# A macaron block on one core: the order of side work in the fourth sums stage, and where its last tiles run

## The chip, the cores and the metric

The kernel runs on one core of one Trainium2 chip. The metric is the device time of one execution in microseconds (us); lower is better. Several executions are timed, and their median counts. One more execution is recorded by the hardware profiler, and the tables and timelines below come from that one.

The engines that matter here are TensorE (matmuls and transposes, PE in the profile), ScalarE (activations and copies, ACT), VectorE (reductions and elementwise work, DVE), GpSimd (indirect DMAs, POOL) and SyncE (which issues most DMAs, SP). Each executes its own instructions in order, and they wait for each other by semaphores.

## The reference, cut to what matters

All is float32. There are four sequences of 512 tokens with 512 channels. A mixture-of-experts layer is applied at half weight, then attention, then the same mixture-of-experts layer again.

```python
def block(x):                                    # x: (4, 512, 512)
    x = x + 0.5 * ffn(layernorm(x))
    x = x + attn(layernorm(x))                   # attn returns out + its input
    return x + 0.5 * ffn(layernorm(x))

def attn(X):                                     # 16 heads of 32 channels
    Xn = layernorm(X) * ln_w + ln_b
    Q, K, V = split(Xn @ W_in, 3)                # rotary embedding on the first 16 channels of Q, K
    probs = softmax(Q @ K.T / sqrt(32))
    return (probs @ V) @ W_out + X

def ffn(x):                                      # x flattened to tokens
    scores = sigmoid(x @ gate_w)                 # 64 experts, 6 chosen by group-limited top-k
    topk_w, topk_ids = grouped_topk(scores + bias)
    y = routed(x, topk_w, topk_ids, w_gate, w_up, w_down)
    shared = (silu(x @ ws_gate) * (x @ ws_up)) @ ws_down
    return y + shared
```

The kernel sends the first expert layer, the attention and the second expert layer through the core one after the other. The change lies in the attention part.

## The kernel before, in words

A tile is 128 tokens, so a sequence has four tiles (`TPB` is 4). The attention of sequence `b` has two stages. The sums stage (`sums`) runs over 4 head groups `c` and 4 query tiles `q`, 16 passes. In each, TensorE computes the scores of four heads into two score buffers (L965), VectorE takes the negated row maximum (`nmq`, L968), and ScalarE takes exponentials whose row sums are accumulated (L973). The results of the exponentials are not kept; only maxima and sums are. `logs` turns the sums into logarithms on VectorE and ScalarE (L944 to L953), and `rows_of_sums` transposes them (`ps_m`, `nmT`). The context stage (`context`) runs over 4 head groups and 4 key tiles `kt`, again 16 passes. TensorE computes transposed scores (L995) and adds the stored rows by a second matmul (L999), ScalarE takes exponentials into `pT` (L1006), and one pass later TensorE multiplies by the values into `cx` (L1018). Score buffers come from `psS`, which has three of two banks each. A sums or a context pass uses two of them.

Beside these passes runs side work. It lies in one queue, `work`, an instance of `Pieces`. A piece is a pair of a weight and a function that issues instructions. A piece with a weight under 1.0 is called short here, another one long. In a sums pass the queue is asked twice. Behind the reductions and ahead of the exponentials, `pieces.short()` takes the piece at the head if it is short. Behind the exponentials, `pieces.long(keep)` takes a short piece at the head and then one more, but only while more than `keep` long pieces are left; the sums stage passes 2 for `keep`. In a context pass, `short()` stands ahead of the exponentials and `long()` behind them, with nothing kept back. `work.all()` issues everything that is left at once. The queue has a second list, `later`, of small VectorE steps; a sums pass flushes one of them, a context pass two.

In the fourth sums stage (`b` is 3) the queue holds, in this order:

- `project(2)`: four long pieces, one per tile. Each is eight matmuls (L860, `po`), an addition on VectorE, and an appended statistics step in `later`. With the last piece, two more steps are appended that turn the statistics into scale and offset (`route.ready`).
- `gated(1, (2, 3))`: the shared expert of the second sequence's tiles 2 and 3. For each tile there is a short piece `turn_h` (transposes of the hidden values on TensorE, copy on ScalarE) and a long piece: the product of the tile before (`route.down`, L508, `so`) and then gate and up (`route.gate`, L208, `gu`, a tanh on ScalarE, two products on VectorE). At the end come `turn_h` and the last `down` with the store.
- `early_rows(2)`: two short pieces that normalise the third sequence's rows 0 and 1 on ScalarE (`route.row`, L295, `xn`) and issue the store of the rows to `xn_d` on SyncE. If the statistics are not there, the piece flushes steps of `later` first.
- `scored(2, chosen)`: the first turn (transposes into `xT`), then `rest`, an empty long piece, then for each tile a turn of the next one and the router's logits (`route.score`, L308, `lg`). Tiles 0 and 1 also issue rows 2 and 3. The last one puts the seven steps of `route.choices` (the choice of experts on VectorE) at the head of `later`.
- `gated(2)`: the shared expert of the third sequence's four tiles.

The transposes, `so`, `gu`, `lg`, `po` and `ps_m` share the pool `psT` of two banks. In the fourth context stage `cx` comes from that pool too (`room` is true). Behind the sums stage, `work.all()` issues what is left; then `queued(2, chosen)` (the token positions of the chosen experts) goes into the queue behind two rests, and `context` begins. Behind the context stage come `project(3)`, the routing of the last sequence, and the second expert layer, whose weights are loaded by SyncE.

The order of instructions on TensorE, ScalarE and VectorE is the order in which the program issues them.

Of the kernel before, what the change touches and what calls it, by code (L numbers as in the profile page):

```python
# [18 lines left out]
B, S, D = 4, 512, 512  # L19
# [64 lines left out]
def macaron_kernel(ctx: ExitStack, tc: tile.TileContext, X, ln_w, ln_b, W_in, W_out, gate_w, bias,  # L84
# [156 lines left out]
    def load_pair(layer, n, extra):  # L241


        slot = (extra if (n + (0 if layer else WS)) % (WS + WX) >= WS else wp).tile([P, 4608], F32, tag="w", name="w")
        wg = slot[:, 0:2 * DC * F].rearrange("p (t c f) -> p t c f", t=2, c=DC)
        wu = slot[:, 2 * DC * F:4 * DC * F].rearrange("p (t c f) -> p t c f", t=2, c=DC)
        wd = slot[:, 4 * DC * F:].rearrange("p (k d) -> p k d", k=3)
        two = slice(2 * n, 2 * n + 2)
        loaded[layer, n] = (wg, wu, wd)
        return [lambda: nc.sync.dma_start(wg, w_gate[two].rearrange("t (p c) f -> p t c f", c=DC)),  # L250
                lambda: nc.sync.dma_start(wu, w_up[two].rearrange("t (p c) f -> p t c f", c=DC)),
                lambda: nc.sync.dma_start(wd, w_down[two].rearrange("t f d -> (t f) d").rearrange("(k p) d -> p k d", p=P))]

    def load_now(*args):
        for go in load_pair(*args):
            go()
# [371 lines left out]
    with ExitStack() as s:  # L628
# [4 lines left out]
        with ExitStack() as f:  # L633
# [35 lines left out]
            rest = [go for n in range(WS + WX) for go in load_pair(0, n, extra)]  # L669
# [58 lines left out]
    with ExitStack() as s:  # L728
# [8 lines left out]
        route = Route(1)  # L737
# [12 lines left out]
        work = Pieces()  # L750

        def places(b):
            qT[b] = qp.tile([P, DC, S], F32, tag="qT", name="qT")
            kT[b] = qp.tile([P, DC, S], F32, tag="kT", name="kT")
            v[b] = vp.tile([P, TPB, D], F32, tag="v", name="v")
# [17 lines left out]
        def summed(b):  # L773

            mv = small.tile([P, TPB, 2], F32, tag="mv4", name="mv")
            for i in range(TPB):
                stat_later(b, mv, i)
            steps_later(first(b, mv))
# [75 lines left out]
        def project(b):  # L854
            mv = small.tile([P, TPB, 2], F32, tag="mv4", name="mv")

            def part(q):
                po = psT.tile([P, 512], F32, tag="ps", name="po")
                for c in range(NC):
                    nc.tensor.matmul(po, lhsT=qT[b][:, c, q * P:(q + 1) * P], rhs=win[3][:, c, :],  # L860
                                     start=c == 0, stop=c == NC - 1)
                nc.vector.tensor_add(xs[b][q], xs[b][q], po)
                if b < B - 1:
                    stat_later(b, mv, q)
                    if q == TPB - 1:
                        steps_later(route.ready(b, mv))
            return [(3.4, lambda q=q: part(q)) for q in range(TPB)]

        def early_rows(b):
            def part(i):  # L870
                while (b, i) not in route.stats:
                    work.flush(1)
                route.row(b, xs[b], i)
            return [(0.1, lambda i=i: part(i)) for i in range(2)]

        rest = (1.0, lambda: None)

        def scored(b, chosen):

            def part(i):  # L880
                route.score(b, i)
                if i + 2 < TPB:
                    route.row(b, xs[b], i + 2)
                if i == TPB - 1:
                    steps = route.choices(b)
                    chosen.append(lambda: next(steps, None))
                    work.later[:0] = chosen * 7

            pieces = [(0.5, lambda: route.turn(b, 0)), rest]
            for i in range(TPB):  # L890
                if i + 1 < TPB:
                    pieces.append((0.5, lambda i=i: route.turn(b, i + 1)))
                pieces.append((1.4, lambda i=i: part(i)))
            return pieces

        def gated(b, tiles=range(TPB)):
            def part(i):
                route.store()
                if i > 0:
                    route.down(b, xs[b], i - 1)  # L900
                route.gate(b, i)

            def last():
                route.down(b, xs[b], TPB - 1)
                route.store()

            pieces = []
            for i in tiles:
                if i > 0:
                    pieces.append((0.3, lambda i=i: route.turn_h(b, i - 1)))  # L910
                pieces.append((4.3, lambda i=i: part(i)))
            return pieces + ([(0.3, lambda: route.turn_h(b, TPB - 1)), (1.7, last)] if TPB - 1 in tiles else [])

        def queued(b, chosen):

            def last():
                while work.later and work.later[0] in chosen:
                    work.flush(1)
                route.store()
                route.count(b)  # L920

            def digits(i):
                if i > 0:
                    route.spread(b, i - 2)
                route.digits(b, i)

            pieces = [(1.0, last)]
            for i in (0, 2):
                pieces += [(0.6, lambda i=i: digits(i)), (1.0, lambda i=i: route.tokens(b, i)), rest]
            pieces.append((0.6, lambda: route.spread(b, 2)))  # L930
            return pieces
# [109 lines left out]
        pieces, following = qkv(0), qkv(1)  # L1041
# [26 lines left out]
        chosen = []  # L1068
        for b in range(B):
            if b > 0:  # L1070
                pieces = project(b - 1)
                if b + 1 < B:
                    places(b + 1)
                    following = qkv(b + 1)
                    pieces.insert(3, following.pop(0))
                    work.add(pieces + following[:-5] + early_rows(b - 1) + following[-5:])
                else:
                    work.add(pieces + gated(b - 2, (2, 3)) + early_rows(b - 1) + scored(b - 1, chosen) + gated(b - 1))
            logs = sums(b, work, 2)
            work.all()  # L1080
            if b + 2 == B:
                load_now(1, 0, None)
            if b == 0:
                summed(2)
                summed(3)
            elif b < B - 1:
                chosen = []
                work.add(scored(b - 1, chosen) + gated(b - 1, range(TPB if b == 1 else 2)) + queued(b - 1, chosen))
            else:
                work.add([rest, rest] + queued(b - 1, chosen))  # L1090
            context(b, work, b in (0, B - 1), logs)
            work.all()
            chosen = []
# [91 lines left out]
```

## Time and profile before

| | us |
|---|---|
| median of 3 runs | 1554.01 (1548.78 to 1554.78) |
| profiled execution, its own time | 1560.13 |
| span of the profile | 1558.4 |
| TensorE busy | 1400.1 (90%) |
| VectorE busy | 625.6 (40%) |
| ScalarE busy | 594.6 (38%) |
| GpSimd busy | 350.7 (23%) |
| mean granted TensorE clock | 0.946 of full speed |

The span runs from the first to the last instruction of one execution; the execution's own time also holds what lies around it. "Busy" is the union of an engine's instructions in time. The granted clock tells which share of full speed TensorE had in a stretch. In a line of a timeline, the numbers are the start, the duration, the engine, the line of the kernel, the operation, the tile written and those read, shapes and count; brackets at the end hold the idle time of the engine just before, and what ended it. In a table by windows, each engine has its busy time and the number of its instructions in brackets; the last three columns are the granted clock, the mean share of the DMA engines in use, and GB/s.

In this execution the fourth sums stage begins at 1008.51 us, the first matmul of the fourth context stage at 1107.60 us, and the last projection's matmuls at 1168.21 us.

### The profile page before, as it was taken

The page shows a single profiled execution, that of the slowest core. Times are in us where ns is not written, and L with a number is a line of the kernel's source. Part 1 is how long each engine was busy: PE and PEld are TensorE (multiplying, and loading weights), DVE is VectorE, ACT ScalarE, POOL GpSimd, SP SyncE. Part 2 cuts the span into 40 slices and gives each one's busy share as a digit, 9 for nine tenths or more (in the row PEclk, how much of TensorE's full clock was granted, in tenths as well). Part 3 has the DMA queues.
Part 4 walks back from the last instruction along what each step waited for, and adds up shares of the span by engine and source line. Part 5 has one row for each costly group of instructions (what it writes and reads, how often), then busy time and mean ns, then how long its engine had stood idle before and what let it go on. Part 6 is the DMA issues. An engine that isn't in the chain of part 4 may idle for free.

```text
span 1558.4 us, 23015 instructions
## 1 busy us (share of the span) xinstructions
PE 1400.1 (90%) x9024; PEld 802.0 (51%) x9024; DVE 625.6 (40%) x1572; ACT 594.6 (38%) x1161; POOL 350.7 (23%) x321
## 2 busy tenths in 40 slices
PE   4785999999998998999999999988998799999990
PEld 4553777776753443333443434335334577777660
DVE  7575222211216575267245842375416422222210
ACT  4431121211111487668635774566452112121120
POOL 2001355554435000000000000000000245555535
PEclk9898899999999997999999999996898899999995
DMA  5477699999999300000000020000006389999989
GB/s 196 144 230 257 184 336 333 328 335 336 341 276 179 115 9 1 1 1 1 28 24 8 1 74 21 4 28 27 24 1 246 118 282 339 337 333 335 329 248 123
DMA packets 127035, 254.57 MB, mean 163 GB/s; under 512 B 15800, under 2 KB 32312, under 8 KB 126928
## 3 DMA queue, kind: packets, MB, share of 16 engines
q1 hardware_dynamic: 87216, 192.96, 35.2%
q0 software_dynamic: 39424, 59.97, 18.0%
q8 instruction: 72, 1.18, 0.3%
q14 instruction: 35, 0.29, 0.1%
q10 hardware_dynamic: 288, 0.16, 0.0%
HBM read 202.21 MB, written 56.95 MB: 166 GB/s over the span
## 4 chain that ended last, share of the span: by engine, by line
PE 56%; ACT 5%; DVE 4%; DMA 2%; issue 2%; POOL 1%; another core or an unknown queue 0%; POOLq 0%; SPq 0%; DVEq 0%; ACTq 0%
PE pq L811 10%; PE gu L549 6%; PE sct L995 5%; PE sc L965 4%; PE cx L1018 4%; PE sct L999 4%; PE ps_t L201 4%; PE eo L568 3%; PE po L860 3%; PE gu L208 3%; PE gu L553 2%; PE so L508 2%; PE eo L571 2%; ACT sc L973 2%; DMA w<-in_L_ffn_w_up_dram 1%
## 5 line engine op out<-in xcount | busy, mean ns | idle before, releaser
L526 POOL DMA_INDIRECT xr<-xn_d,en x128 | 119.5, 934 | 887.3 <-DVE sg L215 716.1
L549 PE MATMUL gu<-bT,w 128*128 128x96 f32 x2048 | 245.5, 278 | 8.3 <-DMA w<-in_L_ffn_w_up_dram 8.3
L549 PEld LDWEIGHTS gu<-bT,w 128*128 128x128 f32 x2048 | 238.5, 195 | 11.6 <-issue 11.5
L973 ACT ACTIVATE sc<-sc,nmq 128x512 f32<-128x512 f32 x256 | 168.9, 660 | 55.7 <-DVE nmq L968 50.0
L811 PE MATMUL pq<-w,lT 128*128 128x512 f32 x384 | 179.6, 615 | 6.6 <-ACT lT L202 2.7
L968 DVE TENSOR_REDUCE nmq<-sc 128x2 f32<-128x1024 f32 x128 | 151.5, 1221 | 74.0 <-PE sc L965 73.8
L576 POOL DMA_INDIRECT total<-ob,en x96 | 138.6, 1443 | 156.3 <-ACT ob L575 120.7
L575 ACT ACTIVATE ob<-eo,xr 96x512 f32<-96x512 f32 x128 | 80.5, 678 | 183.5 <-PE eo L571 180.2
L560 DVE SCALAR_TENSOR_TENSOR sg<-sg,gu 128x288 f32<-128x288 f32 x64 | 29.1, 454 | 301.7 <-ACT sg L559 224.0
L1006 ACT ACTIVATE pT<-sct 128x1024 f32<-128x1024 f32 x128 | 124.1, 1022 | 63.6 <-PE sct L999 63.6
L559 ACT ACTIVATE sg<-gu 128x288 f32<-128x288 f32 x64 | 26.2, 410 | 318.0 <-PE gu L555 318.0
L568 PE MATMUL eo<-w,hT 128*96 128x512 f32 x256 | 125.3, 612 | 0.0
L202 DVE COPY bT<-ps_t 128x384 f32<-128x384 f32 x128 | 65.7, 553 | 144.0 <-PE ps_t L201 121.1
L811 PEld LDWEIGHTS pq<-w,lT 128*128 128x128 f32 x384 | 71.6, 195 | 97.5 <-issue 80.9
L965 PE MATMUL sc<-kT,qT 32*128 32x512 f32 x512 | 93.8, 697 | 8.5 <-ACT sc L973 7.8
L555 PE MATMUL gu<-bT,w 128*64 128x96 f32 x1024 | 98.2, 249 | 0.0
L553 PE MATMUL gu<-bT,w 128*64 128x96 f32 x1024 | 98.2, 249 | 0.0
L995 PE MATMUL sct<-qT,kT 32*128 32x512 f32 x512 | 94.5, 658 | 2.3 <-ACT pT L1006 2.3
L208 PE MATMUL gu<-wsgu,xT 128*128 128x384 f32 x256 | 95.1, 519 | 1.4 <-ACT ob L575 1.4
L553 PEld LDWEIGHTS gu<-bT,w 128*64 128x64 f32 x1024 | 86.2, 137 | 6.0
L999 PE MATMUL sct<-nmT,pick 4*128 4x512 f32 x512 | 88.9, 612 | 0.0
L555 PEld LDWEIGHTS gu<-bT,w 128*64 128x64 f32 x1024 | 86.2, 137 | 0.0
(162 smaller groups left out, 1642.6 us busy)
## 6 DMA issues: line engine op xcount, KB each, us to landing
w<-in_L_ffn_w_gate_dram SPq DMA_DIRECT2D x64, 768.0 KB
w<-in_L_ffn_w_up_dram SPq DMA_DIRECT2D x64, 768.0 KB
w<-in_L_ffn_w_down_dram SPq DMA_DIRECT2D x64, 768.0 KB
total<-zero SPq DMA_DIRECT2D x39, 256.0 KB
xn_d<-xn SPq DMA_DIRECT2D x32, 256.0 KB
x<-in_L_attn_X_dram SPq DMA_DIRECT2D x16, 256.0 KB
x<-total POOLq DMA_DIRECT2D x16, 256.0 KB
out_dram<-x SPq DMA_DIRECT2D x16, 256.0 KB
```

What stands on the lines that cost most here:

```text
L208: nc.tensor.matmul(gu[:rows, :2 * F].rearrange("p (w f) -> p w f", w=2), lhsT=bT[:, c, :], rhs=weights[:, :, c, :], start=c == 0, stop=c = ...
L549: nc.tensor.matmul(g[:, k, :], lhsT=w[:, k, c, f:f + P], rhs=x[:, c, :], start=c == 0, stop=c == DC - 1)
L553: nc.tensor.matmul(g[:FC, 2, :], lhsT=w[:, 0, c, P:F], rhs=xa[:, c, :], start=c == 0, stop=c == DC - 1)
L555: nc.tensor.matmul(g[FC:, 2, :], lhsT=w[:, 1, c, 0:FC], rhs=xb[:, c, :], start=c == 0, stop=c == DC - 1)
L568: nc.tensor.matmul(eos[k][:CAP], lhsT=hT[:, k, :], rhs=wd[:, 2 * k, :], start=True, stop=False)
L576: nc.gpsimd.indirect_dma_start(out=total[layer][k], in_=ob, in_offset=None, out_offset=bass.IndirectOffsetOnAxis(ap=en[:, e:e + 1], axis=0 ...
L811: nc.tensor.matmul(pq, lhsT=lTs[i][:, c, :], rhs=win[n][:, c, :], start=c == 0, stop=c == DC - 1)
L965: nc.tensor.matmul(scs[j // 2][:, j % 2, :], lhsT=qT[b][rows, c, q * P:(q + 1) * P], rhs=kT[b][rows, c, :], start=True, stop=True)
L968: nc.vector.tensor_reduce(nmv[:, q, 2 * pair:2 * pair + 2, c], scs[pair], AX.X, ALU.max, negate=True)
L973: nc.scalar.activation(scs[j // 2][:, j % 2, :], scs[j // 2][:, j % 2, :], AF.Exp, bias=nmq[:, q, j * DH + c:j * DH + c + 1], accum_out=sm ...
L995: nc.tensor.matmul(scs[j // 2][:, j % 2, :], lhsT=kT[b][rows, c, kt * P:(kt + 1) * P], rhs=qT[b][rows, c, :], start=True, stop=False)
L999: nc.tensor.matmul(scs[j // 2][:, j % 2, :], lhsT=pick[rows, c, :], rhs=nmT[b][c // (NC - 1)][rows, :], start=False, stop=True)
```

## The change

Three edits are made, all in the order of the queue for the fourth sums and context stage. First, the two rows of `early_rows` move from behind both tiles of the second sequence to between them, ahead of tile 3's pieces. Second, `scored` gets an argument that leaves out the empty piece behind the first turn; the fourth stage uses it. Third, `work.all()` behind the sums stage is left out for the last sequence, and so are the two empty pieces ahead of `queued`. What the sums stage keeps back then stands at the head of the queue for the context stage. The calls for the other sequences are as before.

```diff
-        def scored(b, chosen):
+        def scored(b, chosen, pause=True):
...
-            pieces = [(0.5, lambda: route.turn(b, 0)), rest]
+            pieces = [(0.5, lambda: route.turn(b, 0))] + [rest] * pause
...
                 else:
-                    work.add(pieces + gated(b - 2, (2, 3)) + early_rows(b - 1) + scored(b - 1, chosen) + gated(b - 1))
+                    work.add(pieces + gated(b - 2, (2,)) + early_rows(b - 1) + gated(b - 2, (3,))
+                             + scored(b - 1, chosen, False) + gated(b - 1))
             logs = sums(b, work, 2)
-            work.all()
+            if b + 1 < B:
+                work.all()
...
             else:
-                work.add([rest, rest] + queued(b - 1, chosen))
+                work.add(queued(b - 1, chosen))
             context(b, work, b in (0, B - 1), logs)
             work.all()
```

## The prediction

> **What bounds the kernel now.** I read the page first (TensorE busy 90% of the span, granted clock 0.946), then the chain of waits (in the fourth sums stage it runs over TensorE's L508 and L208 and ScalarE's L973), then cut the stage into stretches, then read each engine's timeline. "Slot n" is the n-th of the 16 passes (c, q) of the fourth sums stage, counted from 0; it begins at its score matmuls (L965). "Context slot n" is the same for the 16 passes (c, kt) of the stage behind it (L995). The stretches are: slots 5 to 8; 9; 10 to 12; 13 and 14; 15 with the third tile; the fourth tile alone; context slots 0 to 2; the rest.
>
> ```profile
> core 0: us, PE busy (x) PEld busy (x) DVE busy (x) ACT busy (x) POOL busy (x), PEclk, DMA share, GB/s
> 1033.80:1050.10 16.30, 13.29 (x59) 5.16 (x58) 12.70 (x27) 11.53 (x30) 0.00 (x0) 1.00 0.13 49
> 1050.10:1054.20 4.10, 2.17 (x9) 0.58 (x9) 2.35 (x2) 4.03 (x9) 0.00 (x0) 1.00 0.19 68
> 1054.20:1073.40 19.20, 17.88 (x72) 12.37 (x70) 8.38 (x8) 14.60 (x37) 0.00 (x0) 0.50 0.07 27
> 1073.40:1088.70 15.30, 13.09 (x44) 6.12 (x43) 11.06 (x30) 9.27 (x28) 0.00 (x0) 0.84 0.05 18
> 1088.70:1096.40 7.70, 6.06 (x23) 2.68 (x22) 4.68 (x9) 4.29 (x11) 0.00 (x0) 1.00 0.09 35
> 1096.40:1107.60 11.20, 9.02 (x21) 3.96 (x21) 1.40 (x3) 1.07 (x3) 0.00 (x0) 0.85 0.06 24
> 1107.60:1121.40 13.80, 13.54 (x67) 4.59 (x66) 6.49 (x32) 6.05 (x8) 0.00 (x0) 0.67 0.09 30
> 1121.40:1168.20 46.80, 45.47 (x357) 18.29 (x356) 10.11 (x22) 28.23 (x31) 0.00 (x0) 0.99 0.00 1
> ```
>
> No engine is full; the order of the work sets the time. Three places are weak. ScalarE alone carries 1050.10 to 1054.20 (the pause slot). Behind it the clock is halved for all of the score slots. From 1096.40 to 1107.60 the last tile runs with nothing beside it (ScalarE 1.07 of 11.20 us), and then the context stage starts at half clock. TensorE's timeline shows the lone tile:
>
> ```profile
> 1096.41 0.42 PE L201 MATMUL ps_t<-ident,sg 128*96 128x128 f32 x2 [1.20 <-DVE sg L215]
> 1097.29 2.47 PE L508 MATMUL so<-wsd,hT 96*128 96x512 f32 x4 [0.46 <-ACT hT L202]
> 1099.56 3.99 PE L208 MATMUL gu<-wsgu,xT 128*128 128x384 f32 x8
> 1104.75 0.42 PE L201 MATMUL ps_t<-ident,sg 128*96 128x128 f32 x2 [1.20 <-DVE sg L215]
> 1105.68 1.98 PE L508 MATMUL so<-wsd,hT 96*128 96x512 f32 x4 [0.51 <-ACT hT L202]
> ```
>
> The first rows need VectorE's statistics. These lines are VectorE's second half of them (first and last instruction), then ScalarE's row, then TensorE, which waits for it:
>
> ```profile
> 1043.85 0.15 DVE L175 SCALAR_TENSOR_TENSOR c<-rs 128x4 f32<-128x4 f32 x1
> ...
> 1045.03 0.16 DVE L285 SCALAR_TENSOR_TENSOR off<-mv,rs 128x4 f32<-128x4 f32 x1
> ...
> 1045.81 1.25 ACT L295 ACTIVATE xn<-x,off,rs 128x512 f32<-128x512 f32 x1
> ...
> 1047.11 0.66 PE L201 MATMUL ps_t<-ident,xn 128*128 128x128 f32 x4 [1.50 <-ACT xn L295]
> ```
>
> In the kernel before, that half ran in slot 6 and the row in slot 7, so the row found its numbers ready.
>
> **The change, part by part.** I followed the queue of pieces by its own rules (take one short piece behind the reductions; then one long one, with a short one ahead of it, while more than two long ones are left). Before: slots 4 to 6 take the second sequence's tiles 2, 3 and its last product; 7 the rows and the first turn; 8 the pause; 9 to 12 the scores; 13, 14, 15 tiles 0, 1, 2 of the third sequence; tile 3 and the last product run alone. After: 4 takes tile 2; 5 the rows and tile 2's turn; 6 tile 3; 7 the last product; 8 to 11 the scores; 12, 13, 14 tiles 0, 1, 2; 15 only a turn; tile 3 goes into context slot 0, the last product into context slot 1, where the two rests were. So nothing is removed but the pause: every matmul, eviction and store remains.
>
> Slots 0 to 4 do not change, so both start slot 5 at 1033.8. I walked the queues of TensorE, ScalarE and VectorE in program order from there, with durations of this trace.
>
> Slots 5 to 7, after. The row is issued in slot 5, where only the first half of the statistics is done, so the code pulls the second half forward. VectorE: tile products until 1034.97, the slot's two reductions until 1037.2, first half until 1038.4 (six instructions in the trace), second half 1.35 us (1043.85 to 1045.2 above), so 1039.8. ScalarE has waited and now does row 0 (1.15), four exponentials (3.07, from 1036.20 to 1039.27 in the trace), row 1 (1.15), tile 2's copy (0.37): 1045.6. Queued behind row 0 are these exponentials, and TensorE waits for them: slot 6's scores need a score buffer they hold, and tile 3's L508 needs the copy: 1045.9, where in the trace the copy fed L508 at 1035.91. In the 10 us from 1035.7 TensorE has about 2 us of work. That is emptier than the window ahead of 1054.2, so I expect half clock: L508 and L208 take 7.0 instead of 4.5. Slot 7 is 4.2 (the trace's slot 6: 4.06). End 1057.1: 23.3 us. The trace's slots 5 to 8: 16.3. Loss 7.0.
>
> Score slots. Slot 8 no longer waits for a row: scores 1.07, two turns 1.2, L308 1.4, latencies: 3.9. Slots 9 and 10: ScalarE has exponentials 3.07, row 1.15, copy 0.5, tanh 0.1, and TensorE's turn stands in that loop: 6.1 each (trace 6.02). Slot 11: 3.9 (trace's slot 12: 4.54). Together 20.0; trace's slots 9 to 12, 23.3. Gain 3.3.
>
> Tiles to the context stage. After: slot 12 6.0 (still half clock; trace's slot 13 6.4), slot 13 6.9 (like the trace's slot 5, 6.64), slot 14 9.7 (trace 8.92: it waits for the logs), slot 15 1.4: 24.0. Trace's slots 13 to 15 and the lone tile: 34.2. Gain 10.2.
>
> Context slots 0 to 2. Trace: 13.8. After: slot 15's exponentials run until 1105.0, context slot 0's scores share their buffers and end with them; then L508 and L208, in part at half clock: 10.3. In context slot 1 VectorE has the choice's steps ahead of the log, ScalarE's log exponential waits, and the tile's copy stands behind it: 7.1. Context slot 2: 3.5. Together 20.9. Loss 7.1.
>
> Sum: +7.0 -3.3 -10.2 +7.1 = +0.6 us at 1121.4. The rest of the context stage, TensorE-bound at 45.47 of 46.80, just follows. Walked by the same rules the kernel before reaches the end of the stage 3.3 us ahead of its trace, which stays at half clock longer in the context stage; if the new order meets the same, it is +3.9. I take +2.
>
> Two things the trace does not show. Tile 3 and the last product share the two transposition banks with the context's accumulator: between 0 and 2 us (nearest row: L1018 stood 0.5 us behind VectorE's L458); below zero is excluded, as a bank is never freed earlier. I take 0, since each waits for its own predecessor anyway. And row stores go ahead of tile stores on SyncE's queue: each was cleared within the stage, POOL is idle (0.00), and the next weight load is issued at 1183, so 0[...].
>
> **A rule against a row.** The row: 17.88 of 19.20 us busy, granted clock 0.50 throughout. The Trainium skill, TensorE: Matmul & The Clock Gate, "What's actually happening", says that an idle window of about 3.4 us halves the clock and one busy window restores it. Its first half agrees and speaks against the change: slot 5 makes such a hole. Its second half differs: score slots, busy for 93% of the time, did not restore the clock; dense tile matmuls did (the trace's slot 13). By the rule, slots 9 to 12 of the new order are at full clock, 0.5 us less each in three and 1.7 in slot 12, so about -1 us in all. By the row, +2. I take the row.
>
> **Rivals.** (1) Slower: the clock. If the tiles of slots 6 and 7 are too thin, with ScalarE waits between them, to lift it, half clock lasts from slot 6 to slot 13: the last product +1.8, its scores +1.1, slot 8 +2, slot 13 +4.5, about +9.4 on top: 1565. For: seven windows in a row at 0.50 after a smaller hole. Against: tile 3's eight and four matmuls are dense, 4.5 us at full clock. It decides if the window after slot 5's hole is less full than the trace's slot 13. (2) Faster: the gain of the lone tile without the loss. If the hole does not halve the clock (it spares 2.5 in slot 6 and, with the rule, 3 behind it), and tile 3 keeps the context's start at full clock (up to 2.5), it is -6: 1548. For: the lone tile's 11.2 us. Against: the hole is 8 us. (3) Nothing moves: rows earlier, pause and lone tile balance within 0.5 us, 1554; against it, four terms of 3 to 10 us.
>
> **How the numbers follow.** The sum is made against the profiled execution, 1560.13 us (span 1558.4); it lies 6 us above the median of the three runs, so +2 gives 1562 there and 1556.0 on the median 1554.01. Chances: the sum 0.56 (its own range 1550 to 1561), rival 1 0.22, rival 2 0.16, rival 3 0.06. About 0.5%, 7.8 us, is what a measurement of this kernel can tell from no change. Slower by more: most of rival 1 and a tail of the sum, 0.21. Faster by more: half of rival 2, 0.08. Rest 0.71. Range 1547 to 1566.
>
> **What would show it.** Right: in slot 5 VectorE's L175 to L285 directly behind the first half, L295 near 1040, L508 of tile 3 not before 1044, a clock of 0.50 soon after; no lone tile ahead of L995; the context's first three slots about 7 us longer than 13.8. Wrong: L508 of tile 3 near 1040, or slots 6 to 13 all at 0.50, or the stage's end moved by over 8 us.

## The result, and the profile after

| | before | changed |
|---|---|---|
| median of 22 runs each, us | 1551.89 (1546.73 to 1556.52) | 1557.86 (1549.83 to 1567.82) |
| span of the profiled execution, us | 1558.4 | 1555.4 |
| fourth sums stage, first score matmul to first context matmul | 99.1 | 91.3 |
| fourth context stage, to the first matmul of the last projection | 60.6 | 69.2 |
| both, rounded on its own | 159.7 | 160.6 |

The ratio is 1.0047, with a 95% interval from 1.0031 to 1.0064: about 7 us slower, just inside what the forecast called no change. The two profiles alone would say the opposite, since the changed kernel's span is 3 us shorter. That difference lies behind the change. From the last projection to the first output product of the second expert layer (L568, `eo`), before's profile took 80.1 us; in all thirteen later profiles of this study it was 73.9 to 78.8. Within the two stages that the change touches, the first profile after is 0.9 us longer, and a second profile of the same kernel (below, e8) 6.8 us.

This is the table by windows of the changed kernel, cut at its own slots: 5 to 7; 8 to 11; 12 to 15; context slots 0 to 2; the rest of the context stage.

```profile
core 0: us, PE busy (x) PEld busy (x) DVE busy (x) ACT busy (x) POOL busy (x), PEclk, DMA share, GB/s
1034.60:1056.80 22.20, 14.74 (x45) 5.45 (x44) 11.15 (x24) 10.96 (x27) 0.00 (x0) 0.77 0.10 37
1056.80:1077.30 20.50, 17.49 (x81) 11.59 (x80) 10.12 (x9) 16.22 (x40) 0.00 (x0) 0.68 0.10 39
1077.30:1100.70 23.40, 20.09 (x75) 9.04 (x74) 15.96 (x40) 13.62 (x39) 0.00 (x0) 0.92 0.06 23
1100.70:1123.20 22.50, 19.43 (x87) 7.24 (x86) 9.83 (x37) 8.36 (x18) 0.00 (x0) 0.85 0.06 24
1123.20:1169.90 46.70, 45.37 (x357) 17.80 (x356) 10.11 (x22) 29.86 (x33) 0.00 (x0) 1.00 0.02 4
```

The lone tile is gone: the third line holds tiles 0 to 2 with ScalarE at work beside them. What it gave is spent in the first line, where TensorE has 14.74 us of work in 22.20, and in the fourth. Here is the first line's cause, on VectorE, ScalarE and TensorE of the changed kernel:

```profile
1036.26 1.13 PE L965 MATMUL sc<-kT,qT 32*128 32x512 f32 x4
...
1040.46 0.16 DVE L285 SCALAR_TENSOR_TENSOR off<-mv,rs 128x4 f32<-128x4 f32 x1
...
1040.66 1.26 ACT L295 ACTIVATE xn<-x,off,rs 128x512 f32<-128x512 f32 x1 [5.58 <-DVE off L285]
...
1043.38 2.08 PE L965 MATMUL sc<-kT,qT 32*128 32x512 f32 x4 [5.99 <-ACT sc L973]
1046.22 3.78 PE L508 MATMUL so<-wsd,hT 96*128 96x512 f32 x4 [0.76 <-ACT hT L202]
1049.79 3.02 PE L208 MATMUL gu<-wsgu,xT 128*128 128x384 f32 x8
```

ScalarE stood 5.58 us for the last instruction of the statistics (L285). The slot's exponentials queue behind that row, and TensorE waits 5.99 us for a score buffer that they hold. Then L508 takes 3.78 us where it took 1.98, at half clock.

And this is TensorE where slot 15 meets the context stage, in the same kernel:

```profile
1100.36 0.42 PE L201 MATMUL ps_t<-ident,sg 128*96 128x128 f32 x2
1100.71 1.13 PE L995 MATMUL sct<-qT,kT 32*128 32x512 f32 x4
1103.36 0.70 PE L995 MATMUL sct<-qT,kT 32*128 32x512 f32 x2 [1.53 <-ACT sc L973]
...
1105.55 3.78 PE L508 MATMUL so<-wsd,hT 96*128 96x512 f32 x4
1109.12 4.07 PE L208 MATMUL gu<-wsgu,xT 128*128 128x384 f32 x8
```

Slot 15 holds a turn of 0.42 us and nothing else. So the context's first scores come at once, wait 1.53 us for slot 15's exponentials, and the tile behind them starts at half clock: 7.6 us for L508 and L208, which take 4.6 in slot 13.

### The profile page after: what moved, and what is told of

Its sections match the earlier page's. It is cut to its first block, busy times and chain, and to the rows that moved or that the text cites. A ratio compares the mean times of both kernels' runs of the same rounds, so it can differ in the third digit from the quotient of the medians.

```text
span 1555.4 us, 23013 instructions
## 1 busy us (share of the span) xinstructions
PE 1397.3 (90%) x9024; PEld 799.4 (51%) x9024; DVE 626.3 (40%) x1572; ACT 594.7 (38%) x1161; POOL 350.7 (23%) x321
## 4 chain that ended last, share of the span: by engine, by line
PE 55%; ACT 5%; DVE 4%; DMA 4%; issue 2%; POOL 1%; POOLq 0%; SPq 0%; ACTq 0%; DVEq 0%
PE pq L811 10%; PE gu L549 6%; PE sct L995 5%; PE sc L965 4%; PE cx L1018 4%; PE sct L999 4%; PE ps_t L201 3%; PE po L860 3%; PE gu L208 3%; PE eo L568 3%; PE so L508 3%; DMA w<-in_L_ffn_w_up_dram 3%; PE gu L553 2%; PE eo L571 2%; ACT sc L973 2%
## 5 line engine op out<-in xcount | busy, mean ns | idle before, releaser
L576 POOL DMA_INDIRECT total<-ob,en x96 | 138.6, 1443 | 158.4 <-ACT ob L575 114.8
L568 PE MATMUL eo<-w,hT 128*96 128x512 f32 x256 | 125.3, 612 | 0.0
L965 PE MATMUL sc<-kT,qT 32*128 32x512 f32 x512 | 92.9, 693 | 12.1 <-ACT sc L973 11.5
L995 PE MATMUL sct<-qT,kT 32*128 32x512 f32 x512 | 94.6, 659 | 3.5 <-ACT pT L1006 1.9
L208 PE MATMUL gu<-wsgu,xT 128*128 128x384 f32 x256 | 94.5, 517 | 1.4 <-ACT ob L575 1.4
L999 PE MATMUL sct<-nmT,pick 4*128 4x512 f32 x512 | 88.8, 613 | 0.0
```

The costliest lines, as they stand in the source:

```text
L208: nc.tensor.matmul(gu[:rows, :2 * F].rearrange("p (w f) -> p w f", w=2), lhsT=bT[:, c, :], rhs=weights[:, :, c, :], start=c == 0, stop=c = ...
L568: nc.tensor.matmul(eos[k][:CAP], lhsT=hT[:, k, :], rhs=wd[:, 2 * k, :], start=True, stop=False)
L576: nc.gpsimd.indirect_dma_start(out=total[layer][k], in_=ob, in_offset=None, out_offset=bass.IndirectOffsetOnAxis(ap=en[:, e:e + 1], axis=0 ...
L965: nc.tensor.matmul(scs[j // 2][:, j % 2, :], lhsT=qT[b][rows, c, q * P:(q + 1) * P], rhs=kT[b][rows, c, :], start=True, stop=True)
L995: nc.tensor.matmul(scs[j // 2][:, j % 2, :], lhsT=kT[b][rows, c, kt * P:(kt + 1) * P], rhs=qT[b][rows, c, :], start=True, stop=False)
L999: nc.tensor.matmul(scs[j // 2][:, j % 2, :], lhsT=pick[rows, c, :], rhs=nmT[b][c // (NC - 1)][rows, :], start=False, stop=True)
```

## The experiments

All ratios are to the kernel before, run on the same chip in the same rounds. The changed kernel ran beside e5 to e7 (as e8) and not beside the others, so elsewhere it is compared with them by its ratio. The last three columns come from each kernel's one profile, in us, each rounded on its own, and vary from one execution to the next by several us.

| kernel | ratio (95% interval) | sums stage | context stage | both |
|---|---|---|---|---|
| before | | 99.1 | 60.6 | 159.7 |
| changed | 1.0047 (1.0031 to 1.0064) | 91.3 | 69.2 | 160.6 |
| e8, changed once more | 1.0042 (1.0027 to 1.0058) | 91.5 | 75.0 | 166.5 |
| e1, rows back | 1.0004 (0.9982 to 1.0026) | 85.6 | 71.9 | 157.6 |
| e2, rows early only | 1.0046 (1.0027 to 1.0065) | 105.5 | 57.2 | 162.7 |
| e3, statistics early | 1.0015 (0.9990 to 1.0040) | 87.3 | 67.6 | 154.9 |
| e4, leftover only | 0.9984 (0.9965 to 1.0003) | 86.7 | 66.5 | 153.2 |
| e5, rows back, one kept back | 0.9971 (0.9953 to 0.9989) | 90.6 | 64.4 | 155.0 |
| e11, e5 once more | 0.9989 (0.9974 to 1.0005) | 89.9 | 60.6 | 150.5 |
| e6, filler in the hole | 1.0026 (1.0010 to 1.0042) | 90.8 | 67.6 | 158.4 |
| e12, more filler | 1.0024 (1.0008 to 1.0039) | 89.9 | 72.0 | 161.9 |
| e7, pause back | 1.0037 (1.0020 to 1.0054) | 94.8 | 69.1 | 163.9 |
| e9, one kept back | 1.0017 (0.9999 to 1.0034) | 96.3 | 60.6 | 157.0 |
| e10, statistics early, one kept back | 1.0005 (0.9987 to 1.0024) | 92.3 | 62.3 | 154.6 |

**e1: the rows go back.**

```diff
-                    work.add(pieces + gated(b - 2, (2,)) + early_rows(b - 1) + gated(b - 2, (3,))
+                    work.add(pieces + gated(b - 2, (2, 3)) + early_rows(b - 1)
                              + scored(b - 1, chosen, False) + gated(b - 1))
```

> The changed kernel with one part undone: the rows stand behind both tiles of the second sequence again; no pause, and the leftover tile goes into the context stage. Theory H (hole: in slot 5 row 0 waits for the second half of the statistics, TensorE starves for 8 us and its clock halves; the other two parts gain): 3 to 7 us faster than before, about 1547, and L508 of the second sequence's tile 3 waits no longer than 1 us. Theory C (context: the tile in context slots 0 and 1 costs more than it spared, by the log's place behind the choice of experts and by half clock): still 5 us slower than before, about 1557.

The ratio falls from 1.0047 to 1.0004, so the early rows cost the changed kernel about 7 us, and L508 of tile 3 waits 0.46 us and takes 1.98 again:

```profile
1035.96 1.98 PE L508 MATMUL so<-wsd,hT 96*128 96x512 f32 x4 [0.46 <-ACT hT L202]
```

Theory C (the context costs it) is out as the main cause. But H's gain of 3 to 7 us over before did not come either. The other two parts together give nothing that these times can tell, and e1's context stage is 11 us longer than before's, of which the tile that it took over explains a little over half (4.5 us of matmuls and the last product's 2). That pointed to slot 15.

**e2: the rows early, and nothing else.**

```diff
-                    work.add(pieces + gated(b - 2, (2, 3)) + early_rows(b - 1) + scored(b - 1, chosen) + gated(b - 1))
+                    work.add(pieces + gated(b - 2, (2,)) + early_rows(b - 1) + gated(b - 2, (3,))
+                             + scored(b - 1, chosen) + gated(b - 1))
```

> The kernel before with one part alone: the rows between the two tiles of the second sequence; pause kept, last tile run alone ahead of the context stage. Theory H: the hole of about 10 us appears in slot 5, and the kernel is 5 to 8 us slower than before, about 1558. Theory C: within 2 us of before, 1550 to 1554.

7 us slower, as H says. Its window over slots 5 to 7 is the changed kernel's first line again, to a hundredth in TensorE's work and the clock:

```profile
1034.10:1056.30 22.20, 14.74 (x45) 5.42 (x44) 11.14 (x24) 10.95 (x27) 0.00 (x0) 0.77 0.10 37
```

**e3: the statistics ahead of the row.**

```diff
-                    pieces.flush(1)
+                    pieces.flush(3 if (b, c, q) == (B - 1, 1, 0) else 1)
```

> The changed kernel, but slot 4 flushes three of the small steps instead of one, so that the statistics of the third sequence are done before row 0 is issued; nothing else moves. Theory H: TensorE's wait in slot 6 falls from 6 us to under 4, the clock stays at 1.00 through slots 5 to 7, and the kernel is 5 to 8 us faster than the changed one, about 1551. Theory C: as the changed one, 1556 to 1560.

The ratio is 1.0015, some 5 us better than the changed kernel, though its interval still touches the changed kernel's. ScalarE and TensorE of e3:

```profile
1033.55 1.27 ACT L295 ACTIVATE xn<-x,off,rs 128x512 f32<-128x512 f32 x1
1035.93 0.66 ACT L973 ACTIVATE sc<-sc,nmq 128x512 f32<-128x512 f32 x1 [1.11 <-DVE nmq L968]
...
1037.57 1.21 PE L965 MATMUL sc<-kT,qT 32*128 32x512 f32 x4 [1.28 <-ACT sc L973]
1040.41 3.78 PE L508 MATMUL so<-wsd,hT 96*128 96x512 f32 x4 [1.63 <-ACT hT L202]
```

The row no longer waits, TensorE's wait falls from 5.99 to 1.28 us, and slots 5 to 7 take 18.4 us instead of 22.2. One point of H missed: the clock did not stay up. It was at half from 1038.5 to 1045.3, and L508 still takes 3.78 us. Slot 5 has no tile for TensorE whichever way the row is fed; that this is the reason fits e12 below, where filler in that place kept the clock up.

**e4: the leftover alone.**

```diff
             logs = sums(b, work, 2)
-            work.all()
+            if b + 1 < B:
+                work.all()
...
-                work.add([rest, rest] + queued(b - 1, chosen))
+                work.add(queued(b - 1, chosen))
```

> The kernel before with one part alone: what the sums stage keeps back (tile 3 and the last product of the third sequence) runs in context slots 0 and 1 in place of the two rests; rows and pause as before. Theory H: 3 to 5 us faster than before, about 1548, since the 11 us in which the tile ran alone are covered. Theory C: 4 to 7 us slower than before, about 1557.

0.9984: the part is worth about 2.5 us, a little less than H's 3 to 5, and its interval (0.9965 to 1.0003) holds both H's range and no gain at all. Theory C, 4 to 7 us slower, is excluded. With the pause kept, slot 15 carries tile 2, no score matmul waits there, and the tile in context slot 0 runs at full clock.

**e5, e9, e11: one long piece kept back.** The pause was a long piece. With it gone and two still kept back, slot 15 finds none that it may take. These kernels let it take tile 3.

```diff
-            logs = sums(b, work, 2)
+            logs = sums(b, work, 2 if b + 1 < B else 1)
```

> The kernel of e1 (rows back, no pause, leftover in the context stage), but in the fourth stage the queue keeps back one long piece instead of two, so slot 15 carries tile 3 and only the last product goes into the context stage. Theory S (slot 15: with the pause gone one long piece is missing, slot 15 is left with a turn only, its exponentials meet context slot 0's, TensorE thins out and its clock halves there; that eats what the pause gave): from the stage's first score matmul to its last context pass about 153 us where e1 had 157.5, and 2 to 5 us faster than before in time. Rival theory K (the tile costs the same wherever it stands; e1's slow context start was an accident of the clock's phase): as e1, 0 to 1 us from before.

> The changed kernel with one long piece kept back in the fourth stage instead of two (slot 15 carries tile 3; only the last product goes into the context stage); the rows stay early. Theory S (slot 15 is what the missing pause empties): first matmul of the context stage without the wait of 1.5 us for slot 15's exponentials, and 3 to 5 us faster than the changed kernel, ratio to before 0.999 to 1.002. Theory K (the tile costs the same wherever it stands): as the changed kernel, 1.004.

> The fastest version so far (rows back, no pause, one long piece kept back) once more. H and S: ratio to before 0.995 to 0.999, and no slower than the version with early statistics, as rows behind the tiles leave no wait at all. K: 1.000 to 1.002.

e5 is 0.9971 and clear of 1, e11, the same kernel again, 0.9989 with an interval up to 1.0005. Together it is some 3 us faster than before, and the fastest version here. S's 153 us for the two stages came out as 155.0 and 150.5. e9 takes the changed kernel from about 1.0045 (the mean of 1.0047 and 1.0042) to 1.0017, 4 us, as S said, though the intervals touch. TensorE of e11 at the same place:

```profile
1094.60 1.98 PE L508 MATMUL so<-wsd,hT 96*128 96x512 f32 x4 [0.46 <-ACT hT L202]
1096.42 2.75 PE L208 MATMUL gu<-wsgu,xT 128*128 128x384 f32 x8
1099.10 1.14 PE L995 MATMUL sct<-qT,kT 32*128 32x512 f32 x8
1100.06 1.04 PE L999 MATMUL sct<-nmT,pick 4*128 4x512 f32 x8
```

Tile 3 covers slot 15's exponentials, the eight score matmuls run as one block of 1.14 us with no wait, and the context stage takes 60.6 us. e9's does so too. In e5's own profile the context stage took 64.4, as the clock fell to half from 1108 to 1118. In all six profiles without the pause and with two pieces kept back (changed, e8, e1, e3, e6, e12) the clock fell in context slot 0; in the four with one kept back (e5, e9, e10, e11) it did not fall before context slot 2. So a filled slot 15 makes a slow start rarer in these profiles; it does not exclude it.

**e7: the pause comes back.**

```diff
-                             + scored(b - 1, chosen, False) + gated(b - 1))
+                             + scored(b - 1, chosen) + gated(b - 1))
```

> The changed kernel with one part undone: the pause behind the first turn is back, so slot 15 carries tile 2 of the third sequence. Theory S: the pause costs about 3 us in slot 8 and returns about as much at slot 15 and context slots 0 to 2, where no first matmul of the context stage waits for slot 15's exponentials: within 2 us of the changed kernel. Theory P (leaving out the pause is a plain gain): 3 to 6 us slower than the changed kernel, about 1.2% behind before.

1.0037 against 1.0042 for e8 beside it: with or without the pause the time is the same within these intervals, as S says, and P's 3 us and more are just outside. The pause's own slot was a cost: with it, slots 8 to 12 of e7 take 24.4 us where slots 8 to 11 of the changed kernel take 20.5. But context slots 0 to 2 take 16.8 us instead of 22.5. (The rest of e7's context stage took 52.2 us, as the clock fell at 1122.6.) Taking the pause out moved an empty slot from 8 to 15.

**e6 and e12: filler for the clock.** Is the hole's price its length, or the half clock behind it? The filler is dense matmuls whose result nothing reads. The diff is e12's; e6 has only the six behind the long piece.

```diff
+            def filled(n):
+                fill = psT.tile([P, 512], F32, tag="ps", name="fill")
+                for k in range(n):
+                    nc.tensor.matmul(fill, lhsT=ident, rhs=win[3][:, 0, :], start=k == 0, stop=k == n - 1)
...
+                    if (b, c, q) == (B - 1, 1, 2):
+                        filled(3)
                     pieces.long(keep)
+                    if (b, c, q) == (B - 1, 1, 1):
+                        filled(6)
```

> The changed kernel with six dense matmuls more (128x512, about 5 us at full clock), issued behind slot 5's turn, in the hole that row 0 makes; their result is not used. They add work that nothing waits for but slot 6's first scores. Theory H1 (the hole costs mainly by halving the clock): the clock stays at 1.00 until the score slots, tile 3's L508 and L208 take 4.5 us instead of 6.5, and the kernel is 3 to 4 us faster than the changed one. Theory H2 (the hole costs by its length alone): as the changed one or up to 1 us slower.

> The changed kernel with six dense matmuls more behind slot 5's turn and three more in slot 6 ahead of tile 3's product, results unused, so that TensorE has no thin window between slot 5 and slot 8. Theory H1 (the hole costs by halving the clock): clock 1.00 from slot 5 to slot 8, and slot 5 to slot 8 takes 20 us instead of 22.2, 2 us or more off the time. Theory H2 (it costs by its length): 21.5 to 23 us with the clock at 1.00, the same time as the changed kernel within 1 us.

e6 missed its aim: the clock fell at 1039.0 all the same, for one window. In e12 it held. TensorE's timeline of e12:

```profile
1035.49 5.32 PE L958 MATMUL fill<-w,ident 128*128 128x512 f32 x12
...
1043.77 2.84 PE L958 MATMUL fill<-w,ident 128*128 128x512 f32 x6
1046.45 1.88 PE L508 MATMUL so<-wsd,hT 96*128 96x512 f32 x4
1048.17 2.75 PE L208 MATMUL gu<-wsgu,xT 128*128 128x384 f32 x8
```

And its window over slots 5 to 7:

```profile
1034.00:1054.90 20.90, 19.33 (x63) 7.72 (x62) 11.24 (x24) 10.98 (x27) 0.00 (x0) 1.00 0.10 39
```

With the clock at 1.00, slots 5 to 7 take 20.9 us instead of 22.2, though TensorE is busy for 19.33 us instead of 14.74. That lies between H1's 20 and H2's 21.5 to 23. The 1.3 us are not all that half clock costs there: L508 and L208 take 4.5 us instead of 6.6, 2.1 less, but with the filler L508 begins 12.5 us after the start of slot 5 instead of 11.6. So about 2 us of the hole's price are the clock's. The 3.8 us that e3 took off the same stretch are waits: 1.28 and 1.63 us ahead of L965 and L508, instead of 5.99 and 0.76. The time, 1.0024, is some 3 us better than the changed kernel's, with touching intervals. The later falls of the clock come at other places of the work too, so not all of that is put down to slots 5 to 7.

**e8: the changed kernel once more**, and **e10: both faults mended in its own order** (the diffs of e3 and e9 together).

> The changed kernel once more, on the same chip as the others. Theory H: 5 to 9 us slower than before, ratio 1.003 to 1.006; in its profile slot 6's second half of the scores waits 6 us again. Where its execution finds another phase of the clock, the stretch from slot 5 to context slot 3 differs from the first profile's 88.5 us by up to 8 us.

> The changed kernel with both faults mended in its own order: the statistics flushed in slot 4, and one long piece kept back. If H (hole) and S (slot 15) add up: 5 + 4 us faster than the changed kernel, ratio to before 0.996 to 0.999. If only one of them counts: 1.000 to 1.002.

e8 repeats the time (1.0042) and the wait of 5.99 us in slot 6; from slot 5 to context slot 3 it takes 91.8 us where the first profile has 88.5. The table by windows of its profile, context slots 0 to 2 and the rest:

```profile
1098.10:1123.60 25.50, 22.43 (x85) 7.67 (x84) 9.83 (x37) 10.02 (x19) 0.00 (x0) 0.74 0.08 27
1123.60:1173.10 49.50, 48.17 (x358) 18.38 (x357) 10.11 (x22) 28.24 (x31) 0.00 (x0) 0.93 0.00 1
```

TensorE in context slots 1 and 2 of e8:

```profile
1113.78 3.78 PE L508 MATMUL so<-wsd,hT 96*128 96x512 f32 x4 [1.54 <-ACT hT L202]
1117.49 2.09 PE L995 MATMUL sct<-qT,kT 32*128 32x512 f32 x8
```

Each stretch of slots 5 to 15 agrees with the first profile within 0.7 us. The context stage differs by 5.8: the clock fell a second time at the last product and stayed at half to 1130.8. e10 is 1.0005, about 6 us better than the changed kernel and no better than before. The expected 9 us, 0.996 to 0.999, were missed: the mended faults add up only in part. Early rows still leave slot 5 without a tile, which fits: slots 5 to 8 take 21.8 us in e10 and, with the same pieces in the other order, 20.1 in e5 and 18.9 in e11. No run shows it to be the reason.

## Why the prediction was right, and where its size was off

- Direction and range were right; the size was not: +2 us forecast, about +7 measured. The range was wide, from 7 us under the three runs' median to 12 over it. Against the first profile the stretches hold closely, but that the two stages came out at +0.9 where the sum had +0.6 is in part luck: the first stretch was 1.1 us shorter than forecast and the context slots 1.6 longer.

| stretch of the changed kernel | forecast | first profile | second profile (e8) |
|---|---|---|---|
| slots 5 to 7 | 23.3 | 22.2 | 22.9 |
| slots 8 to 11 | 20.0 | 20.5 | 20.0 |
| slots 12 to 15 | 24.0 | 23.4 | 23.4 |
| context slots 0 to 2 | 20.9 | 22.5 | 25.5 |
| rest of the context stage | 46.8 | 46.7 | 49.5 |

- The hole in slot 5 came as described: L285, L295 at 1040.66, L508 at 1046.22, the clock halved from 1040.1 to 1050.4. e2 shows it with nothing else changed, and that alone costs what the whole change costs.
- The terms that were mis-sized are the context slots (+7.1 forecast; 22.5 and 25.5 against before's 13.8 are +8.7 and +11.7) and "just follows" for the rest (up to +2.7). In the first profile it was context slot 0, 12.4 us instead of 10.3; in the second, slots 1 and 2, 8.6 and 6.1 us instead of 7.1 and 3.5, behind a second fall of the clock.
- The trace that the sum was made against was slow as well. It took 1560.13 us, and the median of before's 22 runs is 1551.89. About 4 of these 8 us lie behind the change (80.1 against 76.0 on average in the thirteen later profiles). About 4 more seem to lie in the two stages: the later profiles have 158.2 us there on average, 1.5 under before's 159.7, where their ratios stand for 2.5 us over before on average. So before usually takes about 156 us there. This is an estimate from one profile of each kernel, but the prediction's own walk of before says the same: it ended 3.3 us ahead of the trace. Walk against walk gave +3.9, and only walk against trace gave +0.6. Taking +2 between them halved the better of the two figures.
- The gain of 3.3 us for the score slots was real in the stretch (23.3 to 20.5 and 20.0), but I read the missing pause as a gain of its own. e7 shows none: its other half is the empty slot 15, which the walk listed without seeing the two as one. Nor is the stretch from 1050.10 to 1054.20 of the kernel before the pause slot: slot 8 runs from 1047.69 to 1050.08, and that stretch is the start of slot 9, whose scores wait for slot 8's exponentials. Without the pause the clock fell in slot 9 all the same, at 1064.0.
- Row against rule: the row held. The score slots of both profiles fell to half clock again (granted 0.68 and 0.70 over slots 8 to 11) and stayed there: from 1064.0 to 1077.3 TensorE was busy for 12.5 of 13.3 us at 0.50. The rule's first half fits only in part. In e8 the clock fell at 1038.7, after 3.4 us without any work on TensorE; but in the first profile it fell at 1064.0, after 3.4 us in which TensorE was busy for 1.4.
- Rival 1 (half clock from slot 6 to slot 13) did not happen: the tiles of slots 6 and 7 lifted the clock in both profiles. Rival 2 failed on both its conditions. Rival 3 is out by the ratio itself.

## What to carry to other kernels

When side work is moved earlier in an in-order stage, ask what its operands still wait for, and what is queued behind it on its engine: here one row waiting for VectorE held four exponentials and through them TensorE. Where a scheduler counts pieces, an empty piece is still counted: take it out and some later slot goes empty, so adjust what is kept back in the same step. Walk both orders by the same rules before taking a trace as the baseline: one trace of the kernel before was 8 us slower than its median. And judge a change of a few us by many runs, not by two profiles, because one kernel's two stages together came out as 160.6 and 166.5 us in two executions.

## What the runs showed of the hardware

TensorE's busy share alone does not set the granted clock. In the changed kernel the score slots from 1064.0 to 1077.3 kept TensorE busy for 94% of the time and did not lift a halved clock, while tile matmuls (L508 and L208) lifted it in the hole: L508 began at 1046.22, and the clock was whole again at 1050.4. Two stretches of the kernel before show the same for the fall (columns as in the tables by windows above):

```profile
1085.00:1088.40 3.40, 1.84 (x8) 0.86 (x7) 1.93 (x6) 1.18 (x4) 0.00 (x0) 1.00 0.20 77
1108.90:1112.30 3.40, 3.14 (x24) 1.08 (x16) 3.09 (x21) 1.94 (x2) 0.00 (x0) 1.00 0.20 77
```

In the first, TensorE was busy for 54% of the time, mostly with L208, and the clock stayed whole. In the second it was busy for 92%, with the context's scores (L995 and L999), and the clock was at half from 1112.3 to 1122.5. What in the work counts, no run here isolates. One thin stretch is enough to lose the clock: e6's filler left one between 1034.5 and 1038.2, where only one half of a slot's L965 ran, and the clock fell at 1039.0; with three more matmuls there (e12) it stayed at 1.00 until 1063.3.

In all fourteen profiles the granted clock was 0.50 or 1.00 and nothing between, and every stretch at half was a whole number of steps of 3.41 us long, from one to eight; only the last one, which the end of the execution cuts off, was not. Where these steps fall relative to the work differs from one execution to the next: the clock fell 5.5 us after the start of slot 5 in the changed kernel's first profile and 6.9 us in its second. That this phase decides over several us is my reading of the two profiles of the changed kernel; no run here sets the phase, so it stays open.
